# Transposing x on VectorE and by way of DRAM in a one-core decoder layer

## The chip, the cores and the metric

One NeuronCore of a Trainium2 chip runs the whole program; there is no communication. The metric is the device time of one execution in microseconds; the time of a kernel is the median of its runs. Everything is 32-bit floating point. Engines are named as in the profile: PE is TensorE (PEld its weight loads), DVE is VectorE, ACT is ScalarE, POOL is GpSimd, and SP only issues DMAs.

## What is computed

One decoder layer on x of 16 batches, 512 tokens and 256 channels, in three residual blocks, each closed by a layer norm. The change touches the first:

```python
q  = x + x @ Wq + bq                       # 16 heads of 16 channels
ks = x + x @ Wk[k] + bk[k]                 # k = 0, 1
vs = x + x @ Wv[k] + bv[k]
state = prod over k of (ks[k].T @ vs[k]) / 1024    # per batch and head, 16 x 16
out = LayerNorm(q @ state) @ Wo + bo
x = LayerNorm(x + out)
```

The second block is cross-attention to 64 context tokens with 16 heads; the third is a mixture of eight experts with a capacity of 1024 tokens each, which the inputs give to the first two batches.

## The kernel before, in words

The keys and values of the linear attention are never formed. For each batch the kernel makes the Gram matrix of x over the tokens, with a column of ones beside the channels (`gram`, L544), and gets the states out of it by small products with the weights (`self_attention`, L608: `g_times_wk`, `states`). Tokens lie on the partitions there, so the tile `gx` is x as it stands in memory: four tiles of 128 tokens, 257 columns. Since the Gram matrix sums over tokens, their order within a batch doesn't matter to it. `load_gram_x` (L293) loads it two batches ahead into two buffers; `grams_of` runs up to five batches ahead of the states.

The queries do need x with channels on the partitions. `self_attention(b)` loads x a second time into `xt` (L605) and `transposed` (L227) turns it: eight 128x128 transposes on PE (L233) into two PSUM banks, which ACT and DVE copy out in turn (`evac`, L186 and L188) into `xT`. The query weights and the state are multiplied into one 256x264 matrix `m` (L664, evacuated at L668), and `ps_o` (L681) is x times `m`, token tile by token tile, with the router's columns beside the channels. Norm, another transpose (`zT`, L694), the product with `Wo` (L705), residual and norm follow; `xt` is the residual. `xT` and `zT` take turns in one buffer. The result goes to cross-attention (`ps_sim` L808, softmax over DVE, ACT and POOL, block transposes on DVE at L798, `ps_x` L828) and to the routing.

For the first two batches the experts run as a stream of their own (`ps_h` L940, `ps_e` L957), cut into pieces that fill PE's time from about 200 us on. `ranks` (L869) checks at the end whether later batches belong to the experts as well; they don't here, and the loop at L1151 runs no turns.

The order of the work is written by a planner inside the kernel. Each part is a generator; `Model` (L28) keeps a book of when each tile is made and each engine free by fixed costs per instruction, and `weave` (L1004) always takes the ready stream that is most behind its due time. A `yield WAIT` lets a stream rest until what it issued is done, and `until(...)` until a condition holds. `in_order` (L1023) then fixes this order on PE, DVE, ACT and POOL. DMAs are all issued by SP, which takes its queue in order. PSUM has eight banks of 512 floats, shared by all parts in turn.

Before the steady state lies a setup of some 110 us: the context's keys (`ps_kv` L436, 16 pairs of matmuls whose results go by way of two buffers `st` each to `k_dram`), the values times the output weights (`ps_vo` L486), the router's weights (`ps_rw` L379), and the first four Gram matrices.

Of the kernel before, what the change touches and what calls it, by code (L numbers as in the profile page):

```python
# [9 lines left out]
FP = mybir.dt.float32  # L10
# [3 lines left out]
ALU = mybir.AluOpType  # L14
# [4 lines left out]
P = 128  # L19
# [5 lines left out]
WAIT = "wait"  # L25


class Model:  # L28
# [37 lines left out]
    def run(self):  # L66

        traced = self.nc.cur_bb.bb.instructions
        end = now = self.free.get("PE", 0.0)
        self.took = 0.0  # L70
        for ins in traced[self.seen:]:
            kind, engine = type(ins).__name__, str(ins.engine).split(".")[-1]
            aps = [[a.bass_ap for a in l if hasattr(a, "bass_ap")] for l in (ins.ins, ins.outs)]
            names = [[a.name for a in l] for l in aps]
            at = 0.0
            for made, used, l in ((1, 0, names[0]), (1, 1, names[1])):
                for n in l:
                    if kind == "InstDMACopy" and self.made.get(n, (0, 0))[1] == "SP":
                        continue
                    for known, book in ((made, self.made), (used, self.used)):  # L80
                        if known and n in book:
                            t, by = book[n]
                            at = max(at, t + (self.WIDE.get(by, 0.0) if by != engine else 0.0))
            if kind == "InstDMACopy":
                size = 4 * min(a.size() for l in aps for a in l)
                start = max(at, self.dma if now < 40 else 0.0)
                self.dma = start + size / 220e3
                done = self.dma + 2.0
            elif names[1]:
                start = max(at, self.free.get(engine, 0.0))  # L90
                done = self.free[engine] = start + self.duration(ins, kind, engine)
                if engine == "PE":
                    self.took += done - start
                else:
                    end = max(end, done + 0.15)
            else:
                continue
            for n in names[0] + names[1]:
                self.used[n] = max(self.used.get(n, (0.0, None)), (done, engine), key=lambda p: p[0])
            for n in names[1]:  # L100
                self.made[n] = (done, engine)
        self.seen, self.end = len(traced), end
        return end

# [12 lines left out]
def decoder_layer(  # L117
# [25 lines left out]
    nc = tc.nc  # L143

    B, S, C = x.shape
    J = context.shape[1]
    NT = S // P
    NC = C // P
# [4 lines left out]
    NP = INNER // P  # L153
# [7 lines left out]
    QB = 4  # L161
# [20 lines left out]
    def evac(dst, src):  # L182

        flip[0] ^= 1
        if flip[0]:
            nc.scalar.copy(dst, src)  # L186
        else:
            nc.vector.tensor_copy(dst, src)  # L188
# [30 lines left out]
    w_sel = const.tile([P, NTT, E], FP, tag="w_sel", name="w_sel")  # L219
# [7 lines left out]
    def transposed(dst, src, view=lambda t: t, ones=False):  # L227


        for cc in range(NC):  # L230
            ps = bank("ps_t")
            for t in range(NT):
                nc.tensor.transpose(ps[:, t * P:(t + 1) * P], src[:, t, cc * P:(cc + 1) * P], ident)  # L233
            v = view(dst[:, cc, :])
            ps = ps if len(v.shape) == 2 else ps.rearrange("p (q t i) -> p q t i", q=NT, t=NT)
            if ones and cc == NC - 1:
                nc.vector.tensor_scalar(v, ps, not_last, ident[:, P - 1:P], ALU.mult, ALU.add)
            elif ones:
                nc.scalar.copy(v, ps)
            else:  # L240
                evac(v, ps)

    def moments(NT=NT):

# [27 lines left out]
    with ExitStack() as att:  # L272
# [17 lines left out]
        wk1 = pool(att, "wk1", 1)  # L290
        wk2 = pool(att, "wk2", 2)

        def load_gram_x(b, eng=nc.sync, pieces=1):  # L293

            t = gp.tile([P, NT, C + 1], FP, tag="gx", name="gx")
            nc.gpsimd.memset(t[:, :, C:], 1.0)
            n_ = NT // pieces
            for i in range(pieces):
                eng.dma_start(
                    out=t[:, i * n_:(i + 1) * n_, :C],  # L300
                    in_=x[b, i * n_ * P:(i + 1) * n_ * P, :].rearrange("(t p) c -> p t c", p=P),
                )
            return t

        gram_x = {0: load_gram_x(0, pieces=NT)}
# [138 lines left out]
        def context_keys():  # L444

            cT = held["cT"] = sp.tile([P, NC, BJ], FP, tag="cT", name="cT", bufs=1)
            held["wT"] = {}
            for q in range(BJ // 512):
                transposed(cT[:, :, q * 512:(q + 1) * 512], nats.pop(0))
                nats.append(load_wkv(sp, q))  # L450
                yield WAIT
            for r4 in range(2 * NP // 4):
                nat = nats.pop(0)
                wT = held["wT"][r4] = sp.tile([P, NC, 512], FP, tag="wT", name="wT")
                transposed(wT, nat)
                if r4 + 2 < 2 * NP // 4:
                    nats.append(load_wkv(sp, r4 + 2))
                yield WAIT
                if r4 >= NP // 4:
                    continue  # L460
                for r in range(r4 * 4, r4 * 4 + 4):
                    for q in range(BJ // 512):
                        st = context_rows(r, q)
                        nc.sync.dma_start(
                            out=k_dram[q * NG:(q + 1) * NG, :, r, :].rearrange("g p t -> p g t"),
                            in_=st.rearrange("p (g t) -> p g t", g=NG),
                        )
                        yield
            nc.sync.dma_start(out=xwq, in_=x_wq.rearrange("(r p) c -> p r c", p=P))

            last = small.tile([P, NP], FP, tag="last", name="last")
# [70 lines left out]
        def gram(b, u4):  # L544
# [22 lines left out]
            nc.tensor.transpose(ps[:, :P], g[:, 1, :], ident)  # L567
            evac(g[:, 3, :], ps[:, :P])
            grams[b] = g
            yield WAIT  # L570

        def key_sums(u4):
# [25 lines left out]
                    sums[b // QB][1].append(key_sums(sums["u4"]))  # L598
                    yield WAIT

        grams, sums = {}, {}

        def load_x(b):
            t = wk1.tile([P, NT, CX], FP, tag="xt", name="xt")
# [3 lines left out]
        def self_attention(b, done):  # L608
# [5 lines left out]
            gks = []  # L614

            def g_times_wk(k):

# [36 lines left out]
            state = wk1.tile([P, NC, P], FP, tag="state", name="state")  # L654
            nc.vector.tensor_mul(state, sk[:, 0], sk[:, 1])
            nc.vector.scalar_tensor_tensor(state, state, STATE_SCALE, headmask, ALU.mult, ALU.mult)
            yield from until(lambda: made(xt))
            transposed(xT, xt)
            yield WAIT

            ps = bank("ps_m")
# [11 lines left out]
                )  # L673
            nc.scalar.copy(bq_state[:, :C], ps[:, :C])
            yield WAIT
            z = wk1.tile([P, NT, CX], FP, tag="z", name="z")
            mm = moments()
            for t in range(NT):
                ps = bank("ps_o")
                for cc in range(NC):  # L680
                    nc.tensor.matmul(  # L681
                        ps[:, :CX], xT[:, cc, t * P:(t + 1) * P], m[:, cc, :], start=(cc == 0), stop=(cc == NC - 1)
                    )
                nc.vector.tensor_add(z[:, t, :], ps[:, :CX], bq_state)
                moment(mm, t, z[:, t, :])
                yield
# [182 lines left out]
        def ranks():  # L869
# [36 lines left out]
            least = small.tile([P, NB], FP, tag="least", name="least")  # L906
# [153 lines left out]
        def all_self_attention():  # L1060
            for b in range(B):
                self_st.plan(SETUP + (b - 1) * STEP, STEP, 16.5)
                yield from until(lambda: b in grams and sums[b // QB][1] and "rb" in cs and made(grams[b], sums[b // QB][1][0]))
                yield from self_attention(b, done)

        def all_context():
# [84 lines left out]
    with tc.For_i(0, n, 1) as i:  # L1151
        acc = fw.tile([P, NT, C], FP, tag="acc", name="acc")
        nc.sync.dma_start(out=acc, in_=x2_rest[ds(i * S, S), :].rearrange("(t p) c -> p t c", p=P))
        wb = fw.tile([P, NT, E], FP, tag="wb", name="wb")
        nc.vector.tensor_copy(wb, w_sel[:, ds(i * NT + HEAD_B * NT, NT), :])
        aT = fw.tile([P, NC, S], FP, tag="aT", name="aT")
        transposed(aT, acc)
        for e in range(E):
# [44 lines left out]
```

## Time and profile before

| | |
|---|---|
| median of three runs | 1394.06 us (1392.28 to 1394.08) |
| profiled execution | 1391.12 us |
| its span in the profile | 1389.4 us, 24206 instructions |
| mean granted PE clock | 0.995 of full speed |
| DMA | 153.57 MB in 98373 packets, engines busy 40% |

The profile shows one execution. Busy time is the sum of an engine's instructions; matmuls are pipelined, so their records overlap. A 32-bit matmul has two records, a transpose one. For each group of instructions the page gives line, engine, operation, output<-input, shapes and number, then busy us and the mean ns of one, then the engine's idle time just before them and what ended most of it. Waits are listed by the line that waited and the line that released it.

Of DVE's 850.5 us and ACT's 402.2 us most lies in the softmax, the norms and the evacuations. Of the DMAs, 512 issues of 132 KB load `vo`, the largest share; x is loaded twice, as `gx` and as `xt`, 512 KB a batch each.

### The profile page before, as it was taken

The numbers are of one execution on the slowest core, as the hardware profiler recorded it, in microseconds if no ns is written. First come the engines' busy times: TensorE is split into PE (matmuls) and PEld (weight loads), VectorE is DVE, ScalarE is ACT, GpSimd is POOL, SyncE is SP. The second block draws the span as 40 slices with busy tenths as digits, with TensorE's granted clock in tenths as the row PEclk, the third lists the DMA queues.
The fourth block names the chain that finished last, engine by engine and source line by source line (L and its number), as shares of the span: only waits on it lengthen the run. The fifth ranks groups of instructions, "written<-read, shape, count | busy, mean of one in ns | idle before, by whom it ended". The sixth has DMA issues, their size and how long they took to land.

```text
span 1389.4 us, 24206 instructions
## 1 busy us (share of the span) xinstructions
PE 1363.8 (98%) x9630; PEld 1075.8 (77%) x9630; DVE 850.5 (61%) x1957; ACT 402.2 (29%) x912; POOL 203.9 (15%) x140
## 2 busy tenths in 40 slices
PE   7999999999999999999999999999999999999997
PEld 4666676877878787878878787878888787878686
DVE  2345848466583848476584848475675939484744
ACT  1134323132232314142233223142323323232322
POOL 0001112112020111112020112112020202111200
PEclk9999999999999999999999999999999999999999
DMA  8657775511516153421606053513334061505211
GB/s 261 202 121 193 201 188 169 141 32 33 154 46 157 46 141 106 123 80 47 186 18 169 31 141 106 126 62 75 112 94 124 16 187 46 147 26 126 91 55 40
DMA packets 98373, 153.57 MB, mean 111 GB/s; under 512 B 15561, under 2 KB 70097, under 8 KB 98257
## 3 DMA queue, kind: packets, MB, share of 16 engines
q1 hardware_dynamic: 98256, 151.98, 39.9%
q8 instruction: 78, 1.28, 0.4%
q14 instruction: 39, 0.31, 0.1%
HBM read 114.71 MB, written 37.22 MB: 109 GB/s over the span
## 4 chain that ended last, share of the span: by engine, by line
PE 90%; DVE 6%; DMA 2%; ACT 1%; issue 0%; SPq 0%; DVEq 0%; ACTq 0%
PE ps_x L828 17%; PE ps_sim L808 15%; PE ps_e L957 15%; PE ps_h L940 14%; PE ps_p L705 4%; PE ps_gk L623 4%; PE ps_o L681 3%; PE ps_kv L436 3%; PE ps_t L233 2%; PE ps_vo L486 2%; PE ps_kq L745 2%; PE ps_s L635 2%; PE ps_g L549 2%; PE ps_zt L694 1%; PE ps_m L664 1%; PE ps_g L554 1%
## 5 line engine op out<-in xcount | busy, mean ns | idle before, releaser
L940 PE MATMUL ps_h<-head_T,wi 128*128 128x256 f32 x1024 | 239.1, 379 | 0.0
L828 PE MATMUL ps_x<-vo,pT 32*128 32x264 f32 x4096 | 234.4, 385 | 3.7 <-DVE pT L798 3.7
L808 PE MATMUL ps_sim<-kq,x1T 128*128 128x512 f32 x512 | 235.0, 593 | 0.0
L828 PEld LDWEIGHTS ps_x<-vo,pT 32*128 32x128 f32 x4096 | 212.5, 186 | 24.5 <-issue 5.6
L940 PEld LDWEIGHTS ps_h<-head_T,wi 128*128 128x128 f32 x1024 | 193.4, 190 | 38.8 <-issue 13.0
L796 POOL TENSOR_TENSOR s<-s,sm 128x1024 f32<-128x1024 f32 x64 | 121.8, 1903 | 539.1 <-DVE sm L795 500.7
L835 DVE TENSOR_TENSOR x<-ps_x,x 128x264 f32<-128x264 f32 x64 | 23.2, 426 | 225.6 <-PE ps_x L828 225.6
L816 ACT ACTIVATE s<-s 128x512 f32<-128x512 f32 x128 | 80.7, 630 | 276.0 <-DVE s L815 276.0
L808 PEld LDWEIGHTS ps_sim<-kq,x1T 128*128 128x128 f32 x512 | 94.5, 190 | 83.2 <-issue 74.2
L814 DVE TENSOR_REDUCE mx<-ps_sim 128x8 f32<-128x512 f32 x128 | 86.1, 672 | 42.2 <-PE ps_sim L808 41.9
L815 DVE TENSOR_TENSOR s<-ps_sim,mx 128x512 f32<-128x512 f32 x128 | 88.5, 692 | 4.4
L719 POOL TENSOR_TENSOR x<-x,bout 128x1056 f32<-128x1056 f32 x16 | 38.8, 2422 | 320.9 <-ACT hT L946 172.6
L798 DVE STREAM_TRANSPOSE pT<-s 128x1024 f32<-128x1024 f32 x64 | 78.6, 1228 | 7.0 <-POOL s L796 7.0
L946 ACT ACTIVATE hT<-ps_h 128x256 f32<-128x256 f32 x128 | 47.0, 377 | 119.9 <-PE ps_h L940 119.7
L695 ACT ACTIVATE zT<-ps_zt,shift,gain 128x512 f32<-128x512 f32 x32 | 23.2, 776 | 189.7 <-PE ps_zt L694 189.7
L794 DVE TENSOR_REDUCE sm<-s 128x16 f32<-128x1024 f32 x64 | 77.1, 1204 | 0.4 <-ACT s L816 0.4
L267 ACT ACTIVATE x<-x,off,rstd 128x264 f32<-128x264 f32 (+1 forms) x112 | 58.3, 591 | 29.3 <-DVE off L265 29.3
L681 PE MATMUL ps_o<-m,xT 128*128 128x264 f32 x256 | 66.7, 387 | 0.0
L261 ACT ACTIVATE rstd<-bn_mv,eps 128x4 f32<-128x4 f32 (+1 forms) x70 | 20.7, 295 | 158.6 <-DVE bn_mv L250 155.1
L948 DVE TENSOR_SCALAR hT<-ps_h 128x256 f32<-128x256 f32 x128 | 52.1, 409 | 22.5 <-PE ps_h L940 22.3
L705 PE MATMUL ps_p<-wo,zT 128*128 128x264 f32 x256 | 63.1, 387 | 0.0
L436 PE MATMUL ps_kv<-cT,wT 128*128 128x512 f32 x128 | 61.1, 612 | 0.2 <-ACT vst L186 0.2
(172 smaller groups left out, 1892.6 us busy)
## 6 DMA issues: line engine op xcount, KB each, us to landing
vo<-vo_dram SPq DMA_DIRECT2D x512, 132.0 KB, 4.1
vo_dram<-vst SPq DMA_DIRECT2D x128, 132.0 KB, 2.4
xt<-in_x_dram SPq DMA_DIRECT2D x16, 512.0 KB, 4.0
wi<-L_ffn_experts_inter_dram SPq DMA_DIRECT2D x8, 1024.0 KB, 5.1
gx<-in_x_dram SPq DMA_DIRECT2D x15, 512.0 KB, 4.2
x_rest<-x SPq DMA_DIRECT2D x14, 512.0 KB, 3.0
out_dram<-x SPq DMA_DIRECT2D x14, 512.0 KB, 2.9
k_dram<-st SPq DMA_DIRECT2D x16, 256.0 KB, 3.5
```

The lines of the kernel that those rows point to most:

```text
L436: nc.tensor.matmul(ps, wT[:, cc, r % 4 * P:(r % 4 + 1) * P], cT[:, cc, q * 512:(q + 1) * 512], start=(cc == 0), stop=(cc == NC - 1),)
L681: nc.tensor.matmul(ps[:, :CX], xT[:, cc, t * P:(t + 1) * P], m[:, cc, :], start=(cc == 0), stop=(cc == NC - 1))
L705: nc.tensor.matmul(ps[:, :CX], zT[:, cc, t * P:(t + 1) * P], wo[:, cc, :], start=(cc == 0), stop=(cc == NC - 1))
L796: nc.gpsimd.tensor_mul(s, s, sm.unsqueeze(2).to_broadcast([P, NH, J]))
L798: nc.vector.transpose(probsT[:, :, t, :], s.rearrange("p h (a j) -> p (h a) j", a=2))
L808: nc.tensor.matmul(ps, x1T[:, cc, t * P:(t + 1) * P], kq[:, cc, hf * 512:(hf + 1) * 512], start=(cc == 0), stop=(cc == NC - 1),)
L814: nc.vector.tensor_reduce(mx[:, hs], sim, AX.X, ALU.max)
L815: nc.vector.tensor_sub(s[:, hs, :], sim, mx[:, hs].unsqueeze(2).to_broadcast([P, 8, J]))
L816: nc.scalar.activation(s[:, hs, :], s[:, hs, :], AF.Exp, scale=SCALE)
L828: nc.tensor.matmul(ps[q][:, :CX], probsT[pq, blk].rearrange("p t i -> p (t i)"), vos[c][pq, i, :], start=(c == 0 and i == 0), stop=(c == 7 ...
L940: nc.tensor.matmul(ps[:, :TB], wi[:, cc, f * P:(f + 1) * P], head_T[b][:, cc, t0 * P:t0 * P + TB], start=(cc == 0), stop=(cc == NC - 1),)
L957: nc.tensor.matmul(ps[:, :C], hT[f][:, t * P:(t + 1) * P], wo_[:, f, :], start=(f == 0), stop=(f == NF - 1),)
```

## The change

`w_sel` is dropped (its values go into `w_all`), which together with single buffers for `last` and `least` makes room for a tile `xb`. For batch 0 everything else stays. For batches 1 to 15:

- `gx` is loaded in another order of tokens, by four DMAs of 32 partitions each instead of one of 128.
- Behind the batch's Gram matrix DVE transposes `gx` in 32x32 blocks (`to_blocks`, four instructions), and ACT issues a DMA of the blocks to a DRAM tile `x_blocks[b]`. Only then is the next `gx` loaded into the same pair of buffers.
- `self_attention(b)` begins with four DMAs, issued by ACT (`from_blocks`), that read the blocks into `xT` with channels on the partitions. PE's transposes of `xt` and their two evacuations are gone; `xt` is still loaded for the residual.
- `ps_o` reads `xT` in another layout, and waits in the plan until it is there.
- The planner's book reckons 0.35 us of ACT for a DMA issue of ACT and 5 us until it has landed.

```diff
@@ Model.run
-            if kind == "InstDMACopy":
+            if kind == "InstDMACopy" and engine == "Activation":
+                start = max(at, self.free.get(engine, 0.0))
+                self.free[engine] = start + 0.35
+                done = start + 5.0
+            elif kind == "InstDMACopy":
@@ new
+    def to_blocks(src):
+        xb = wk1.tile([P, NT, NC, NT, 32], FP, tag="xb", name="xb")
+        for q in range(NT):
+            nc.vector.transpose(
+                xb[:, :, :, q, :].rearrange("p k c j -> p c k j"),
+                src[:, q, :C].rearrange("p (c k j) -> p c k j", c=NC, j=32),
+            )
+        return xb
+
+    def from_blocks(dst, there):
+        for k in range(NT):
+            nc.scalar.dma_start(
+                out=dst[k * 32:(k + 1) * 32].rearrange("i t c n -> i t (c n)"),
+                in_=there[:, :, k, :].rearrange("t i n -> i t n"),
+            )
@@ load_gram_x
+                else:
+                    eng.dma_start(
+                        out=t[i * 32:(i + 1) * 32, :, :C],
+                        in_=x[b, i * P:(i + 1) * P, :].rearrange("(q j) c -> j q c", j=32),
+                    )
@@ gram
-            if b + 2 < B:
-                gram_x[b + 2] = load_gram_x(b + 2)
...
             grams[b] = g
+            if b > 0:
+                yield WAIT
+                xb = to_blocks(gx)
+                yield WAIT
+                x_blocks[b] = dram.tile([NT, 32, NT, NC * P], FP, tag=f"x_blocks{b}", name="x_blocks")
+                nc.scalar.dma_start(
+                    out=x_blocks[b].rearrange("t i k n -> (t i) (k n)"), in_=xb.rearrange("p k c q j -> p (k c q j)")
+                )
+            if b + 2 < B:
+                gram_x[b + 2] = load_gram_x(b + 2)
@@ self_attention
-            xT = wk1.tile([P, NC, S], FP, tag="xT", name="xT")
+            xT = wk1.tile([P, NT, NC, P], FP, tag="xT", name="xT")
+            if b > 0:
+                from_blocks(xT, x_blocks.pop(b))
...
-            yield from until(lambda: made(xt))
-            transposed(xT, xt)
+            if b == 0:
+                yield from until(lambda: made(xt))
+                transposed(xT.rearrange("p t c n -> p c t n"), xt, lambda t: t)
...
+            yield from until(lambda: made(xT))
...
-                        ps[:, :CX], xT[:, cc, t * P:(t + 1) * P], m[:, cc, :], start=(cc == 0), stop=(cc == NC - 1)
+                        ps[:, :CX], xT[:, t, cc], m[:, cc, :], start=(cc == 0), stop=(cc == NC - 1)
@@ ranks
-            nc.vector.scalar_tensor_tensor(w_sel, rank, float(CAP), w_all, ALU.is_lt, ALU.mult)
+            rest = slice(HEAD_B * NT, NTT)
+            nc.vector.scalar_tensor_tensor(
+                w_all[:, rest], rank[:, rest], float(CAP), w_all[:, rest], ALU.is_lt, ALU.mult
+            )
```

Since every part is planned anew, instructions far from these lines stand in another order too.

More of the change, by code (lines that the diff above doesn't have):

```diff
@@ L98, in run @@
             for n in names[0] + names[1]:
-                self.used[n] = max(self.used.get(n, (0.0, None)), (done, engine), key=lambda p: p[0])
+                by = "SP" if kind == "InstDMACopy" else engine
+                self.used[n] = max(self.used.get(n, (0.0, None)), (done, by), key=lambda p: p[0])
             for n in names[1]:
-                self.made[n] = (done, engine)
+                self.made[n] = (done, "SP" if kind == "InstDMACopy" else engine)
         self.seen, self.end = len(traced), end
@@ L218, in decoder_layer @@
     NTT = B * NT
-    w_sel = const.tile([P, NTT, E], FP, tag="w_sel", name="w_sel")
     n_i = const.tile([P, 1], I32, tag="n_i", name="n_i")
@@ L234, in transposed @@
             v = view(dst[:, cc, :])
-            ps = ps if len(v.shape) == 2 else ps.rearrange("p (q t i) -> p q t i", q=NT, t=NT)
+            if len(v.shape) > 2:
+                ps = ps.rearrange("p (q n) -> p q n", n=P) if len(v.shape) == 3 else ps.rearrange(
+                    "p (q t i) -> p q t i", q=NT, t=NT
+                )
             if ones and cc == NC - 1:
@@ L291, in decoder_layer, with load_gram_x @@
         wk2 = pool(att, "wk2", 2)
-        def load_gram_x(b, eng=nc.sync, pieces=1):
+        def load_gram_x(b, eng=nc.sync, pieces=NT):
             t = gp.tile([P, NT, C + 1], FP, tag="gx", name="gx")
@@ L298, in load_gram_x @@
             for i in range(pieces):
[L299 to L302, printed above, removed]
+                if b == 0:
+                    eng.dma_start(
+                        out=t[:, i * n_:(i + 1) * n_, :C],
+                        in_=x[b, i * n_ * P:(i + 1) * n_ * P, :].rearrange("(t p) c -> p t c", p=P),
+                    )
+                else:
+                    eng.dma_start(
+                        out=t[i * 32:(i + 1) * 32, :, :C],
+                        in_=x[b, i * P:(i + 1) * P, :].rearrange("(q j) c -> j q c", j=32),
+                    )
             return t
@@ L469, in context_keys @@
             nc.sync.dma_start(out=xwq, in_=x_wq.rearrange("(r p) c -> p r c", p=P))
-            last = small.tile([P, NP], FP, tag="last", name="last")
+            last = small.tile([P, NP], FP, tag="last", name="last", bufs=1)
             nc.vector.tensor_copy(last, xwq[:, :, C - 1])
@@ L569, in gram @@
             grams[b] = g
+            if b > 0:
[5 more added lines that the diff above has]
+                    out=x_blocks[b].rearrange("t i k n -> (t i) (k n)"), in_=xb.rearrange("p k c q j -> p (k c q j)")
+                )
+            if b + 2 < B:
+                gram_x[b + 2] = load_gram_x(b + 2)
             yield WAIT
@@ L599, in grams_of @@
                     yield WAIT
-        grams, sums = {}, {}
+        grams, sums, x_blocks = {}, {}, {}
         def load_x(b):
@@ L612, in self_attention @@
             sk = wk1.tile([P, K, NC, P], FP, tag="sk", name="sk")
-            xT = wk1.tile([P, NC, S], FP, tag="xT", name="xT")
-            gks = []
+            xT = wk1.tile([P, NT, NC, P], FP, tag="xT", name="xT")
+            if b > 0:
+                from_blocks(xT, x_blocks.pop(b))
             def g_times_wk(k):
@@ L656, in self_attention @@
             nc.vector.scalar_tensor_tensor(state, state, STATE_SCALE, headmask, ALU.mult, ALU.mult)
-            yield from until(lambda: made(xt))
-            transposed(xT, xt)
+            if b == 0:
+                yield from until(lambda: made(xt))
+                transposed(xT.rearrange("p t c n -> p c t n"), xt, lambda t: t)
             yield WAIT
@@ L903, in ranks @@
             nc.vector.tensor_add(rank, rank, start)
-            nc.vector.scalar_tensor_tensor(w_sel, rank, float(CAP), w_all, ALU.is_lt, ALU.mult)
+            rest = slice(HEAD_B * NT, NTT)
+            nc.vector.scalar_tensor_tensor(
+                w_all[:, rest], rank[:, rest], float(CAP), w_all[:, rest], ALU.is_lt, ALU.mult
+            )
             NB = B - HEAD_B
-            least = small.tile([P, NB], FP, tag="least", name="least")
+            least = small.tile([P, NB], FP, tag="least", name="least", bufs=1)
             nc.vector.tensor_reduce(
@@ L1062, in all_self_attention @@
                 self_st.plan(SETUP + (b - 1) * STEP, STEP, 16.5)
-                yield from until(lambda: b in grams and sums[b // QB][1] and "rb" in cs and made(grams[b], sums[b // QB][1][0]))
+                yield from until(
+                    lambda: b in grams and sums[b // QB][1] and "rb" in cs and made(grams[b], sums[b // QB][1][0])
+                    and (b == 0 or b in x_blocks and made(x_blocks[b]))
+                )
                 yield from self_attention(b, done)
@@ L1154, in decoder_layer @@
         wb = fw.tile([P, NT, E], FP, tag="wb", name="wb")
-        nc.vector.tensor_copy(wb, w_sel[:, ds(i * NT + HEAD_B * NT, NT), :])
+        nc.vector.tensor_copy(wb, w_all[:, ds(i * NT + HEAD_B * NT, NT), :])
         aT = fw.tile([P, NC, S], FP, tag="aT", name="aT")
```

## The prediction

> **What bounds the kernel now.** I read the page's busy times first, then the grid of slices, then who TensorE waited for, then TensorE's timeline around the transposes in question, then the setup in windows.
>
> ```profile
> PE 1363.8 (98%) x9630; PEld 1075.8 (77%) x9630; DVE 850.5 (61%) x1957; ACT 402.2 (29%) x912; POOL 203.9 (15%) x140
> PEclk9999999999999999999999999999999999999999
> ```
>
> TensorE works for all but 25.6 of 1389.4 us; no other engine comes near. So an instruction taken off TensorE shortens the run by its own length, unless something else is then late. The waits filtered to TensorE say how close that is:
>
> ```profile
> PE ps_x L828 <- DVE pT L798: 3.7, 2, 3.2
> PE ps_rw L379 <- DVE early L376: 3.3, 1, 3.3
> PE ps_t L233 <- DMA nat<-in_L_xattn_Wkv_dram: 3.1, 1, 3.1
> PE ps_g L549 <- DMA gx<-in_x_dram: 3.0, 1, 3.0
> PE ps_e L957 <- DVE hT L948: 1.8, 1, 1.8
> ```
>
> (columns: total us, times, longest.) Three of the five, 9.4 us, lie in the first 32 us; behind it there is hardly a wait. The stages from 200 us to 1300 us are filled by the planner with expert matmuls, so there a microsecond off TensorE counts in full. TensorE's timeline around one transposition of x:
>
> ```profile
> 229.53 1.03 PE L940 MATMUL ps_h<-head_T,wi 128*128 128x256 f32 x4
> 230.40 1.04 PE L233 MATMUL ps_t<-ident,xt 128*128 128x128 f32 x8
> 231.27 3.60 PE L808 MATMUL ps_sim<-kq,x1T 128*128 128x512 f32 x8
> ```
>
> The records overlap, so the price is start to start: 231.27 - 230.40 = 0.87 us for eight. Fourteen of the sixteen batches show 0.86 to 0.89, the first two 0.96.
>
> **Removed.** For batches 1 to 15 the eight transposes go: 120 instructions. The built order of the changed kernel has exactly 120 fewer matmuls, all of this kind, and as many changes between 128, 64 and 32 rows as before (81), so nothing is added at the seams. 14 x 0.87 + 0.96 = 13.1 us off TensorE. Their evacuations also go, 15 on DVE and 15 on ACT:
>
> ```profile
> L188 DVE COPY xT<-ps_t 128x512 f32<-128x512 f32 x16 | 10.9, 683 | 0.0
> L186 ACT COPY xT<-ps_t 128x512 f32<-128x512 f32 x16 | 9.2, 575 | 3.2 <-PE ps_t L233 3.2
> L798 DVE STREAM_TRANSPOSE pT<-s 128x1024 f32<-128x1024 f32 x64 | 78.6, 1228 | 7.0 <-POOL s L796 7.0
> ```
>
> **Added on VectorE.** 60 block transposes of 128x256. The nearest row is the last one: 1228 ns for 1024 elements, also written with a stride; taking 80 ns of it as fixed, 256 elements cost 0.37 us. 60 x 0.37 - 15 x 0.68 = +12 us on an engine with 539 us idle. They stand behind the Gram matrices, several batches ahead of need; the cover is DVE's idle third. Without cover four in a row delay what stands behind them by 1.5 us.
>
> [...]
>
> **Added in DMA.** Per batch one write of 512 KB and four reads of 128 KB, 15 MB on 153.57 MB: the DMA share goes from 40% to about 44%. The reads are issued at the start of self_attention(b) and first needed by ps_o. Adding up the matmuls between in the built order at their rows gives 15 us in the three tightest batches and 23 to 35 in the others, against about 4 us for the comparable loads (xt 4.0, gx 4.2 from issue to landing). Hidden; with the cover gone it is 4 us a batch.
>
> **Added in ACT's queue.** The write and the reads are issued by ACT, 75 issues. No DMA issue on ACT is in the trace; the nearest row is SP's: 0.39 us alone, 17.56 / 32 = 0.55 in a burst of vo loads. So 75 x 0.39 to 0.55 = 29 to 41 us, less 15 x 0.575 = 9 us of copies: ACT goes from 29% to about 31%. What matters is the block of four reads, 1.6 to 2.2 us, with kq copies, Exp or hT queued behind it. [...] By the row it is half the landing time, on an engine that computes. In the built order TensorE reaches ps_e 3.5 to 5 us of matmul work after the hT that ACT evacuates, and the planner already reckons 0.35 us an issue, so an overrun of some 0.6 us should mostly be absorbed. From 0 (all absorbed) to 5 us (a third of a microsecond per batch); a gain is excluded, since copies worth 0.6 us leave and 2.0 to 2.75 us come. I take 1, near the absorbed end.
>
> Each DMA also takes one of eight landing counters in turn and waits until that counter's previous DMA, possibly SP's, has landed. In the built order no such wait hangs on later TensorE work than ACT has already waited for; the closest (batch 2, behind the xt load) leaves 4.9 us of matmuls for a landing of 4.0.
>
> **Moved: the loads of gx.** For b > 0 four issues instead of one: 45 more on SP, and they now wait for DVE's transposes as well as for ps_g. Later gx loads are needed tens of microseconds on; queued behind them are vo loads with 9 us of reserve. In the setup it is tighter. Windows of 6 us:
>
> ```profile
> 6.00:12.00 6.00, 5.38 (x35) 4.23 (x34) 1.65 (x7) 1.77 (x4) 0.10 (x1) 1.00 1.10 338
> 12.00:18.00 6.00, 2.86 (x20) 2.21 (x19) 2.06 (x6) 0.64 (x2) 0.11 (x1) 1.00 1.03 345
> 24.00:30.00 6.00, 3.87 (x10) 1.39 (x8) 1.23 (x2) 0.78 (x2) 0.00 (x0) 1.00 0.97 283
> 30.00:36.00 6.00, 4.83 (x13) 3.56 (x14) 1.13 (x5) 0.00 (x0) 0.00 (x0) 0.72 0.63 167
> ```
>
> (PE, PEld, DVE, ACT, POOL busy; clock; DMA share; GB/s.) The DMA engines are full where TensorE waits for nat, so three more issues before it (3 x 0.51 us) delay it by 0 to 1.5, taken 1.0: the issue is late, but the transfers are the limit. ps_rw waits for DVE, which sits behind k_dram stores; the new order puts 8 ps_kv instead of 6 before it, four transposes into DVE's queue and gx behind them into SP's, ahead of two stores: -0.5 (two more matmuls cover) to +3, taken 1.0. The fourth Gram matrix has 6.6 us of matmuls for four issues and a landing of 4.2 behind two stores: 0 to 2, taken 0.5. Sum 2.5 us, from -0.5 to 6.5. A longer wait here costs twice: the last window shows the clock at 0.72 after the 3.3 us wait.
>
> **Moved: everything else.** The planner decides again. In the new order four places take a PSUM bank with little work since it was used (a kq or g copy 0.2 to 1.1 us of matmuls earlier, where the copy alone is 0.28 to 0.68 us and queues): about 0.5 us each, 2 us, from -3.7 (the pT waits could vanish) to 5; I take 2 because the places can be named. At the end, DVE's rank sums delay hT (1.8 us); the new order has 14 ps_h matmuls instead of 10 between ps_in and that wait, 1.7 us more cover: -0.7, from -1.5 to 0. w_sel's merging into w_all is one instruction, slightly shorter: nothing.
>
> **Sum.** -13.1 + 1 + 2.5 + 2 - 0.7 = -8.3 us. The profiled execution took 1391.1 us, 1.7 outside its span; this would be 1382.8. The runs' median is 1394.06, 2.9 above the profiled one, so on the median 1394.06 - 8.3 = **1385.8 us**.
>
> **The rivals.** Under 0.2% (2.8 us) a measurement of this kernel cannot be told from no change.
>
> *Nearly all of the gain arrives* (0.18): the re-planned order costs nothing, the setup's extra issues lie in the shadow of full DMA engines. -13.1 - 0.7 = 1380.3. For it: TensorE has no wait worth the name from 200 to 1300 us. Against it: the tight banks.
>
> *The setup eats it* (0.12): nat, ps_rw and the Gram load at their upper ends, 6.5 us with the clock penalty of 1.6, and the banks at 4: -13.1 + 8.1 + 4 = -1.0, 1393.1. For it: the setup is where waits are; against: only 35 us of it.
>
> *ACT's queue becomes the bound* (0.08, slower): at the four reads of self_attention(b), ACT waits for another DMA's landing, 4.1 us, and then issues, 2.75: 6.9 us in which no bank is emptied by ACT. TensorE's reserve is about 4.3, so it loses 2.6 us; in every second batch 7 x 2.6 = 18 us, 1385.8 + 18 = 1404. From (8.3 + 2.8) / 15 = 0.74 us per batch on, the change is slower than before. For it: a computing engine now waits in order on DMAs. Against: the built order has them landing long before.
>
> The forecast itself has 0.62, its own range 1380.5 to 1391. That the transposes stay is excluded by the built order.
>
> **How the numbers follow.** Faster 0.80 (the forecast and the full gain), same 0.12, slower 0.08. The range, 1378.5 to 1394.5, takes in the bounds of the unknown terms except their coinciding, the full gain, and the case of the setup; above it lies ACT's case.
>
> **What would show it.** ps_t<-ident,xt in one batch only; TensorE's busy time down by about 15 us as its records count (each 1.04 us a group, overlapping); 60 transposes into xb near 370 ns; DMA issues on ACT near 0.4 to 0.55 us; TensorE's waits at 20 to 26 us, more of them before 40 us. Wrong if TensorE waits for hT, kq or s of ACT by more than 5 us in total, if ps_o waits for xT, or if SP stands behind gx while ps_x waits for vo.

## The result, and the profile after

The changed kernel takes 1405.29 us (median of six runs, 1403.26 to 1409.26); beside it the kernel before took 1393.52 us. The ratio is 1.0092, 95% interval 1.0074 to 1.0109: 12.8 us slower by the ratio (11.8 by the two medians), where 8.3 us faster was forecast, and outside the range. The profiled execution took 1404.68 us (before 1391.12), its span is 13.6 us longer.

The page of the changed kernel, busy times and granted clock:

```profile
PE 1360.0 (97%) x9510; PEld 1065.4 (76%) x9510; DVE 849.9 (61%) x2002; ACT 395.5 (28%) x897; POOL 203.6 (15%) x140
PEclk9999998999999999999999999999999999999999
```

TensorE has 120 instructions fewer, but only 3.8 us less busy time, and it is idle for 43.0 us instead of 25.6. Busy time counts overlapping records once, so 13.1 us less were due, and not the 15 that the forecast got by adding up the records. The slice with clock 8 (210 to 245 us) lies in the stage in which most of the new idle time arose. Whom TensorE waited for (total us, times, longest):

```profile
PE ps_g L583 <- DMA gx<-in_x_dram: 5.3, 2, 3.1
PE ps_t L237 <- ACT x L294: 3.9, 4, 3.4
PE ps_vo L520 <- ACT vst L191: 3.5, 5, 1.9
PE ps_rw L413 <- DVE early L410: 3.5, 1, 3.5
PE ps_vo L520 <- DVE s L860: 3.1, 3, 2.0
PE ps_gt L599 <- ACT g L191: 3.0, 1, 3.0
PE ps_gt L599 <- DVE g L193: 2.4, 1, 2.4
```

The waits for gx and ps_rw lie before 40 us, the wait for g of DVE at 350 us; of the others all but 0.4 us lie between 150 and 250 us: with 0.7 us for x_head 13.8 us, where the kernel before had 2.2. What follows such waits stands in the windows of 10 us there (PE, PEld, DVE, ACT, POOL busy; clock; DMA share; GB/s):

```profile
220.00:230.00 10.00, 6.53 (x33) 5.40 (x32) 8.02 (x28) 1.92 (x7) 0.10 (x1) 1.00 0.85 196
230.00:240.00 10.00, 5.73 (x19) 3.61 (x20) 2.38 (x9) 4.89 (x12) 2.40 (x1) 0.57 1.06 249
240.00:250.00 10.00, 10.00 (x30) 6.04 (x29) 6.36 (x14) 1.15 (x2) 0.00 (x0) 0.91 0.87 235
```

After 3.5 us of idle the clock is 0.57 in the next window: of the 5.7 us that look busy there some 2.5 (5.73 x 0.43, an estimate) are the same matmuls taking longer. Added up over windows of 5 us, busy time times what is missing of the full clock, the clock costs 8.9 us in the changed kernel and 4.2 before. These 4.7 us are half of the 9.3 by which busy time fell short; the other half stays open (in e3 below, where only the transposes are gone, it falls short by 3.4).

What the change touches itself looks as forecast: the transposes of xt are there for batch 0 only (eight), the block transposes take 412 ns, a DMA issue of ACT 0.34 us for a write and 0.44 for a read, and the landings (last column of the page's DMA rows, us) are short:

```profile
L257 DVE STREAM_TRANSPOSE xb<-gx 128x256 f32<-128x256 f32 x60 | 21.2, 412 | 2.8 <-DMA x_blocks<-xb 2.8
x_blocks<-xb ACTq DMA_DIRECT2D x15, 512.0 KB, 3.1
xT<-x_blocks ACTq DMA_DIRECT2D x60, 128.0 KB, 3.1
```

The simplest landmark is the start of ps_x, which comes once per batch. How much later than before TensorE reaches it, in us, worked out from the traces (some of the runs below are in the table too). Each row is one profiled execution, and executions of one kernel differ: 45 of the kernel before lay between 1388.2 and 1395.5 us, the one profiled of e5 is 2.2 us above the median of its kernel, that of e6 3.8 below. The runs e1 to e18 are described in the next section:

| kernel | batch 0 | 1 | 4 | 8 | 15 |
|---|---|---|---|---|---|
| changed | 13.0 | 22.3 | 18.5 | 19.5 | 11.4 |
| old order, no transposes (e3) | 1.2 | 1.1 | -1.3 | -4.7 | -9.7 |
| new order alone (e5) | 13.9 | 17.6 | 12.8 | 13.8 | 5.0 |
| new order, no trip (e1) | 16.9 | 22.8 | 18.0 | 19.0 | 10.9 |
| old order, no trip (e6) | 1.5 | 4.1 | 3.1 | -0.4 | -5.4 |
| old order, all new work (e4) | 5.0 | 14.6 | 18.1 | 15.6 | 11.7 |
| old order, from batch 8 (e13) | 1.5 | 2.2 | 3.4 | 1.7 | -2.3 |

The changed kernel is 22.3 us late at batch 1. From there to batch 15 it makes up 10.9 us, as the one with the bare transposes left out does (10.8), but 2.6 us of that (an estimate from the rows of ps_h) are not a gain: 12 matmul records of the experts that stood ahead of ps_x of batch 15 now stand behind it. At batch 1 what is done otherwise weighs about the same (16 expert records more, 16 Gram records fewer). So some 8.3 of the 10.8 us arrive, about three quarters; TensorE's idle time between the two landmarks is 6.9 us instead of 3.7, the 2.4 us of the wait for g at 350 us among it.

### The profile page after: what moved, and what is told of

It is laid out like the page before. It is cut to its first block, busy times and chain, and to the rows that moved or that the text cites. A ratio compares the mean times of both kernels' runs of the same rounds, so it can differ in the third digit from the quotient of the medians.

```text
span 1403.0 us, 24179 instructions
## 1 busy us (share of the span) xinstructions
PE 1360.0 (97%) x9510; PEld 1065.4 (76%) x9510; DVE 849.9 (61%) x2002; ACT 395.5 (28%) x897; POOL 203.6 (15%) x140
## 4 chain that ended last, share of the span: by engine, by line
PE 83%; DVE 8%; DMA 5%; SPq 2%; ACT 1%; issue 1%; POOL 0%; DVEq 0%; ACTq 0%; POOLq 0%
PE ps_x L873 15%; PE ps_h L988 14%; PE ps_e L1005 14%; PE ps_sim L853 13%; PE ps_p L750 4%; PE ps_gk L666 4%; PE ps_o L726 3%; PE ps_kv L470 3%; PE ps_kq L790 2%; PE ps_vo L520 2%; PE ps_s L678 2%; PE ps_g L583 1%; PE ps_t L237 1%; DVE pT L843 1%; DVE sm L839 1%; SPq L525 1%
## 5 line engine op out<-in xcount | busy, mean ns | idle before, releaser
L666 PE MATMUL ps_gk<-wk,g 128*128 128x256 f32 x256 | 61.8, 388 | 0.0
```

What stands on the lines that cost most here:

```text
L666: nc.tensor.matmul(ps[:, :C], blk, wk[:, j, k, :], start=(j == 0), stop=(j == NC - 1))
```

## The experiments

The planner answers to any edit with another order, so an edit of the source changes two things at once. To change one, the planner's choices were written down (which stream goes next, and whether a condition held) and replayed in another kernel. "New order" is that of the changed kernel, "old order" that of the kernel before:

```diff
         def weave():
             model.run()
-            while streams:
-                ...
-                st = min(now, key=Stream.time)
-                wait = next(st.gen, "end")
+            every = list(streams)
+            for i in range(0, len(PICKS), 2):
+                known = len(streams)
+                st = every[int(PICKS[i:i + 2], 16)]
+                wait = next(st.gen, "end")
+                model.run()
+                every += streams[known:]
```

"us" below is the ratio to the kernel before on the same chip less 1, times 1393. A difference of two rows carries both intervals, some 2 to 4 us together; the terms below are to be read so. In e1, e3, e5, e6, e15, e17 and e18 part of the work is left out.

| run | ratio (95%) | us |
|---|---|---|
| changed kernel | 1.0092 (1.0074 to 1.0109) | +12.8 |
| e1 new order, no trip | 1.0075 (1.0058 to 1.0092) | +10.4 |
| e2 new order, trip by SP | 1.0114 (1.0082 to 1.0146) | +15.9 |
| e3 old order, no transposes | 0.9906 (0.9889 to 0.9922) | -13.1 |
| e4 old order, all new work | 1.0105 (1.0082 to 1.0128) | +14.6 |
| e5 new order alone | 1.0018 (1.0011 to 1.0025) | +2.5 |
| e6 old order, no trip | 0.9991 (0.9981 to 1.0002) | -1.3 |
| e7 from batch 4, planned | 1.0089 (1.0066 to 1.0112) | +12.4 |
| e8 from batch 4, old order | 1.0033 (1.0021 to 1.0045) | +4.6 |
| e9 from batch 7, old order | 1.0012 (1.0003 to 1.0021) | +1.7 |
| e10 from batch 7, planned | 0.9989 (0.9980 to 0.9999) | -1.5 |
| e11 before, replanned a | 1.0057 (1.0039 to 1.0075) | +7.9 |
| e12 before, replanned b | 1.0007 (0.9993 to 1.0022) | +1.0 |
| e13 from batch 8, old order | 0.9972 (0.9963 to 0.9980) | -3.9 |
| e14 from batch 8, planned | 0.9974 (0.9966 to 0.9982) | -3.6 |
| e15 new order, one step moved | 1.0034 (1.0022 to 1.0045) | +4.7 |
| e16 old order, trip by SP | 1.0078 (1.0060 to 1.0096) | +10.9 |
| e17 gx in pieces alone | 0.9953 (0.9939 to 0.9966) | -6.5 |
| e18 block transposes alone | 0.9947 (0.9929 to 0.9965) | -7.4 |

### Is it ACT's queue, or the order? (e1 to e4)

From the waits two theories could be read: ACT, which now issues DMAs and waits for landings (A), or the new order (B). Without the trip:

```diff
-                nc.scalar.dma_start(
-                    out=x_blocks[b].rearrange("t i k n -> (t i) (k n)"), in_=xb.rearrange("p k c q j -> p (k c q j)")
-                )
...
-                from_blocks(xT, x_blocks.pop(b))
...
-                        ps[:, :CX], xT[:, t, cc], m[:, cc, :], start=(cc == 0), stop=(cc == NC - 1)
+                        ps[:, :CX], xT[:, t, cc] if b == 0 else xt[:, t, cc * P:(cc + 1) * P], m[:, cc, :],
+                        start=(cc == 0), stop=(cc == NC - 1),
```

> The changed kernel with every engine's order kept as planned, but without the trip by way of DRAM: the write of x_blocks and the four reads of xT (75 DMA issues on ACT, 15 MB) are left out, and ps_o takes the untransposed x for batches 1 to 15, so its values mean nothing. VectorE's block transposes, the pieces of gx and their order stay. Theory A, ACT's queue: issues on ACT wait for landings and hold up the evacuations behind them; then without them the time falls by nearly all of the missing 20 us, to 1385 to 1390. Theory B, the order: the planner's new order leaves TensorE without ready work in the setup and from 150 to 250 us, whatever ACT issues; then only the one wait of 3.0 us for g behind ACT's issue and its clock dip go, and the time is 1398 to 1402.

Measured +10.4 us (1403.8), just above the range of B. The trip costs 2.4 us in the new order, which the two intervals do not tell from nothing. A falls for the changed kernel. With `nc.sync` instead of `nc.scalar` for the trip:

> The changed kernel with the orders of TensorE, VectorE, ACT and POOL kept, but the write and the reads of the trip are issued by SP instead of ACT. Theory A (ACT's queue): ACT is free, about 1386 to 1392, unless SP's own queue becomes late. Theory B (the order): 1399 to 1406, since TensorE's waits for DVE and for the setup stay.

+15.9 us: no gain from an ACT free of issues. Now the bare price, the old order with `transposed(xT, xt)` for batch 0 only, and ps_o reading xt as above:

> The kernel before, every engine's order kept, with TensorE's transposes of x for batches 1 to 15 and their evacuations simply left out: ps_o takes the untransposed x, so its values mean nothing. This is the price of the removed part alone. Both theories: 13.1 us less than before, 1381; if other waits take up part of it, up to 1386.

-13.1 us, the sum of the transposes (with an interval of 2.3 us to either side, the last digit is luck). All the new work in the old order, without yields and conditions of its own:

```diff
-                yield WAIT
                 xb = to_blocks(gx)
-                yield WAIT
...
-            yield from until(lambda: made(xT))
```

> All of the change's work (block transposes on VectorE, the trip issued by ACT, gx in four pieces behind them), in the order in which the planner of before put the rest: the new instructions stand where their step stood, and the order of the others is that of the kernel before. Theory A (ACT's queue): the issues on ACT still hold up the evacuations, 1396 to 1405. Theory B (the order): 1382 to 1389, the removed transposes less some small waits.

+14.6 us (1405.7), at the upper end of A's range, so B fails in its pure form too: in the old order the change is as slow as in the new one, by another way. Its trace shows how. First ACT's timeline (start, duration; in brackets the idle time before):

```profile
221.71 0.34 ACTq L653 DMA_DIRECT2D x_blocks<-xb  x1
222.10 0.30 ACT L336 ACTIVATE rstd<-bn_mv,eps 128x4 f32<-128x4 f32 x1 [2.59 <-DMA vo<-vo_dram]
```

ACT's write has its data and stands still until a vo load, issued by SP, has landed; g is evacuated behind it, and TensorE waits 2.4 us for g. Then SP's queue and TensorE:

```profile
225.22 7.92 SPq L381 DMA_DIRECT2D gx<-in_x_dram  x8
234.22 0.45 SPq L1067 DMA_DIRECT2D wi<-L_ffn_experts_inter_dram  x1
241.26 1.76 PE L1033 MATMUL ps_h<-head_T,wi 128*128 128x256 f32 x4 [5.00 <-DMA wi<-L_ffn_experts_inter_dram]
```

Eight pieces of gx stand ahead of the first expert's weights. The second four come behind VectorE's block transposes, which wait 1.2 us for ACT's write to land, since xb has one buffer; SP itself waits 4.4 us among them for other landings (2.3 for gx, 2.1 for xT). Before, wi was issued at 220.35 us; here at 234.22, and the first expert matmul waits 5.0 us.

### Splitting the sum (e5, e6, e17, e18, e16)

The new order with none of the new work (the trip is left out as in e1, and gx comes in the token order of before):

```diff
-        def load_gram_x(b, eng=nc.sync, pieces=NT):
+        def load_gram_x(b, eng=nc.sync, pieces=1):
...
+            if b + 2 < B:
+                gram_x[b + 2] = load_gram_x(b + 2)
             g = gp.tile([P, 4, P], FP, tag="g", name="g", bufs=5)
...
                 yield WAIT
-                xb = to_blocks(gx)
                 yield WAIT
...
-            if b + 2 < B:
-                gram_x[b + 2] = load_gram_x(b + 2)
```

> The changed kernel's order alone: every engine keeps the order that the planner chose for the change, but VectorE's block transposes, the trip by way of DRAM and the pieces of gx are left out; gx is loaded by one DMA right after its Gram matrix, as before. As in the runs without transposes ps_o takes the untransposed x, so its values mean nothing. Theory B (the order itself leaves TensorE waiting; the run without the trip, 1404, still held it): 1398 to 1404. Theory C (the block transposes, and gx loaded in pieces behind them, are what delays): 1380 to 1385, as the kernel before without its transposes (1380).

+2.5 us (1395), between the two expectations. Against -13.1 for the old order, the order costs 15.6 us; neither B nor C is the whole. The old order with transposes and pieces but no trip:

> The old order with the block transposes and the pieces of gx, but without the trip by way of DRAM (ps_o takes the untransposed x, so its values mean nothing). With the trip this order took 1406. Theory C (transposes and pieces): 1398 to 1404. Theory D (in an order that was planned without it, the trip's issues on ACT cost some 20 us; the new order avoids that and loses as much by its own waits): 1381 to 1387.

-1.3 us (1391), between C and D. Transposes and pieces cost 11.8 us in the old order and 7.9 in the new (e1 less e5); the trip 15.9 in the old (e4 less e6) and 2.4 in the new. The sum for the changed kernel is -13.1 + 15.6 + 7.9 + 2.4 = 12.8 us; it closes by construction, since each term is the difference of one run and the next. In the planner's order the trip is cheap and the order dear; in the old one it is the other way round.

The pieces alone (four DMAs, other token order, issued where the one was), and the block transposes alone (one DMA in token order, behind them):

> The old order without transposes of x (1380), with one part of the change added: gx of batches 1 to 15 comes in four pieces and in the other token order, issued where it was, right after its Gram matrix. No block transposes, no trip, and ps_o takes the untransposed x, so its values mean nothing. With the block transposes too it took 1391. If the pieces in SP's queue cost those 11 us: 1387 to 1391. If the block transposes and the loads behind them do: 1380 to 1383.

> The other part alone: the old order without transposes of x, with the block transposes on VectorE, and gx loaded by one DMA in the order of before, but behind them, as in the change. Values mean nothing here either. If the pieces cost the 11 us: 1380 to 1384. If the block transposes and the load (with its memset on POOL) moved behind them do: 1385 to 1391.

6.6 and 5.7 us more than e3: together 12.3, against 11.8 for both. Neither part carries the price alone. By the ps_x landmark the pieces have lost their share by batch 1 (6.0 us late, e3 1.1); the transposes lose theirs between batch 0 (1.9 us early, e3 1.2 late) and batch 2 (2.3 late, e3 0.2). Of the 5.7 us for the transposes, 2.5 are one wait of TensorE for `off` of VectorE at 252 us, the wait that in e9 follows a VectorE instruction of 2.19 instead of 0.19 us beside GpSimd (last section), with the clock at 0.66 in the 5 us behind it. Every old-order run with block transposes of batch 7 has this wait (e4, e6, e8, e9, e16, e18), and e3, e13 and e17 don't.

> All of the change's work in the old order (1406 with the trip issued by ACT, 1391 without the trip), with the write and the reads issued by SP. If the trip's 15 us in this order are ACT's, which waits for landings with g and Exp behind it: 1390 to 1395. If they are SP's and the DMA engines' (expert weights and vo late): 1402 to 1409.

+10.9 us (1401), near the second expectation: ACT's part of the trip's 15.9 is 3.7 us. Most of the other 12.2 is again the late wi, whoever issues the trip: it is issued at 234.64 us, TensorE waits 6.1 us for it, and in the 7 us behind that the clock is 0.51, another 3.4 us.

### What in the new order costs (e15), and whether any new order does (e11, e12)

VectorE's timeline of the new order alone (e5), the end of batch 0's softmax:

```profile
178.34 1.10 DVE L244 COPY vst<-ps_vo 128x264 f32<-128x264 f32 x3
...
185.99 1.77 DVE L244 COPY vst<-ps_vo 128x264 f32<-128x264 f32 x4 [4.44 <-PE ps_vo L571]
187.68 1.24 DVE L889 STREAM_TRANSPOSE pT<-s 128x1024 f32<-128x1024 f32 x1
188.83 1.18 DVE L885 TENSOR_REDUCE sm<-s 128x16 f32<-128x1024 f32 x1
...
199.86 0.43 DVE L244 COPY vst<-ps_vo 128x264 f32<-128x264 f32 x1 [5.06 <-DMA vo_dram<-vst]
...
202.30 1.24 DVE L889 STREAM_TRANSPOSE pT<-s 128x1024 f32<-128x1024 f32 x1
```

and the same steps in the old order (e3):

```profile
176.93 1.21 DVE L848 STREAM_TRANSPOSE pT<-s 128x1024 f32<-128x1024 f32 x1
178.06 1.18 DVE L844 TENSOR_REDUCE sm<-s 128x16 f32<-128x1024 f32 x1
...
189.46 1.23 DVE L848 STREAM_TRANSPOSE pT<-s 128x1024 f32<-128x1024 f32 x1
```

In the new order eight evacuations of value products stand in VectorE's queue ahead of the last row sum and the last two pT. They wait for TensorE, whose clock is 0.50 from 180 to 185 us, and later ones for stores to land, while softmax data lies ready: the last row sum comes 10.8 us later, the last pT 12.8 us, and ps_x of batch 0 starts at 204.40 instead of 191.71 us. 2.1 us of this shift are eight more value products done by then; the rest is lost. In the whole span TensorE is idle for 35.9 us in e5 and for 25.4 in e3, and the clock, added up as above, costs 10.8 and 5.6 us: 10.5 + 5.2 us, which is the order's price within the spread of single executions. By batch 1 nearly all of it has been lost (16.5 us, with as much work done).

Another reading was that TensorE lacks work in reserve: the old order has eight value products left behind ps_x and ps_p, the new none, and it waits there for x. One step was moved, in the replayed list:

```diff
- ps_vo (last), ps_x, ps_p, ...
+ ps_x, ps_p, ps_vo (last), ...
```

> The run of the new order alone (1395; no transposes of x, no trip, no block transposes, its values mean nothing) with one step moved: the last eight value products (ps_vo, 2.1 us) go from before the first ps_x to behind ps_p, where the old order had them. In the new order TensorE has only ps_p and a Gram matrix, 6.8 us, between ps_x and the transposes of x that need its result, and waits 2.6 us with a clock dip behind it. If the lack of such work in reserve is what the new order loses by: 1389 to 1393. If the place of this step does not matter: 1394 to 1397.

+4.7 us, not less than e5: that reading falls. ps_x now waits 2.56 us for pT instead. This agrees with the chain through VectorE as the limit of the stage. That the chain is the cause is read from the traces and not shown by a run: moving the softmax steps themselves was not tried.

Is the new order bad, or is nearly any? The kernel before, with one constant of the planner's book altered:

```diff
-            return 0.09 + n * 1.035e-3 ...
+            return 0.10 + n * 1.035e-3 ...
```

> The kernel before, with all its work and nothing added; only the planner reckons 0.10 us instead of 0.09 us as the fixed part of each VectorE instruction, so it chooses another order in 15 places before 430 us and more behind. If almost any other order of the crowded stage is worse than the one before had: 1397 to 1408. If the order of the change was bad by itself, and not orders in general: 1390 to 1395.

> The kernel before with all its work; only the planner reckons 0.13 us instead of 0.11 us for a transpose on TensorE, so it chooses another order in 22 places before 430 us. Expected as for the other one: 1397 to 1408 if almost any other order is worse, 1390 to 1395 if the order of the change was bad by itself.

(In the second a transpose is reckoned at 0.13 us instead of 0.11.) +7.9 and +1.0 us with the work unchanged: one order as in the first expectation, one as in the second (and not clear of nothing: its interval runs from -1.0 to 3.1 us). From batch 4 on the planned order costs 7.8 us more than the old one (e7 less e8). So a re-plan that reaches the first 360 us cost 1.0, 7.8, 7.9 and 15.6 us in the four orders measured.

### Where the change pays (e7 to e10, e13, e14)

With `b > 0` replaced by `b >= LATE`, and earlier batches as before:

> The change for batches 4 to 15 only, planned anew by the planner: batches 1 to 3, whose Gram matrices belong to the setup, keep TensorE's transposes and the single load of gx. 12 x 0.87 = 10.4 us less on TensorE. If the losses lie in the setup and in the stage from 150 to 250 us that it disturbs (B or C there): 1383 to 1388. If each batch loses through ACT's queue (A): 1396 to 1403.

> The same change for batches 4 to 15, in the order of the kernel before. If the trip's issues on ACT cost wherever the order was not planned for them (D): 1394 to 1402. If only the setup and batches 1 and 2 suffer (C, or D in that stage alone): 1383 to 1388.

+12.4 us, worse than either expectation, and +4.6, as D: the stage that loses (150 to 360 us) already works on the Gram matrices of later batches, up to batch 7, so the setup's batches are not all that it touches.

> The change for batches 7 to 15 only, in the order of the kernel before: the first Gram matrix with a trip is reached near 430 us, behind the stage from 150 to 360 us in which all losses of the runs so far lie. 9 x 0.87 = 7.8 us less on TensorE. If the work itself is free where the experts' matmuls fill the gaps: 1384 to 1387. If each trip costs ACT or SP something in the steady stage too: 1390 to 1394.

> The same change for batches 7 to 15, planned anew: the planner's order is that of the kernel before up to about 430 us and differs behind it. If a new order hurts only where there are no experts to fill in: 1384 to 1388. If any new order costs (some 10 us, as in the first 360 us): 1393 to 1400.

+1.7 us, at the upper expectation, and -1.5, between the two: a gain of 7.8 nearly lost. By the landmark e9 is 4.1 us late at batch 1 and 7.1 at batch 2, and then makes up. Its first block transposes lie at 339 us and not near 430, as was expected, and at 254 us a VectorE instruction of 0.19 us takes 2.19 (last section).

> The change for batches 8 to 15 only, in the old order. With batch 7 in it, one block transposition and its write fell at 339 us and a moved memset on POOL at 252 us held up VectorE by 2 us, both in the crowded stage; from batch 8 on everything new lies behind 360 us. 8 x 0.87 = 7.0 us less on TensorE. If the crowded stage is where all losses lie: 1385 to 1388. If the steady stage pays too: 1390 to 1394.

> The same for batches 8 to 15, planned anew. The planner's choices up to some 430 us are those of before. If the crowded stage is where all losses lie, also those of a new order: 1385 to 1388. If a new order costs in the steady stage too: 1390 to 1396.

-3.9 and -3.6 us, with intervals below 1: both are faster than the kernel before, by about half of the 7.0 us. Behind the crowded stage most of it arrives: by the landmark e13 gains 5.7 us from batch 6 to batch 15 (3.4 late, 2.3 early), with the order of the other work as before and one new wait of 0.6 us, for kq near 919 us. e14 moves from 3.9 late to 3.1 early, but 16 expert records, some 3.4 us, have gone behind ps_x of batch 15, so its gain is about 3.6. Ahead of it, with one load of gx in pieces as the only new work, the two executions are 3.4 and 3.9 us late; how much of that is the spread of single executions these runs don't tell.

## Why the prediction was wrong

- **-13.1 us for the transposes: right.** -13.1 measured (e3). In the changed kernel about three quarters of it arrive behind batch 1 (8.3 of 10.8 us).
- **"Moved: everything else", 2 us, from -3.7 to 5: this step failed.** The new order alone costs 15.6 us (e5 less e3), by some 10.5 us of idle TensorE and 5.2 of lower clock, while the prediction reckoned with a lower clock in the setup only. The prediction looked in the built order for places where a PSUM bank is taken soon after its last use, and priced four of them at 0.5 us. It did not follow VectorE's queue in the stage from 150 to 250 us, where the steady state's cover, the expert matmuls, does not yet exist; the last pT comes 12.8 us later there. "From 200 us to 1300 us filled by the planner" was taken as cover for everything outside the setup; expert matmuls begin at 229.5 us before and at 252.5 in the changed kernel.
- **VectorE's transposes "hidden", gx and the setup 2.5 us, from -0.5 to 6.5: mis-sized.** Together 7.9 us in the new order and 11.8 in the old. The 0.37 us of one was nearly right (0.41), though its 80 ns of fixed time were an assumption; what the trace of before shows is that VectorE's records overlap by 80 ns (902 of 952 overlaps, to the nearest 10 ns). Half of the price are the pieces (6.6 us), half the transposes with the load and its memset behind them (5.7, both in the old order), of which 2.5 us are the wait for `off` at 252 us (in e9 with GpSimd's memset moved away), which no term had. Of the three waits named for the setup only one grew: ps_g from 3.0 to 5.3 us. ps_rw went from 3.3 to 3.5 and nat from 3.1 to 1.6, in single executions. The cover named for the transposes, VectorE's idle third, is an average over the span: VectorE is busy for 27.95 of the 30 us from 150 to 180 us in e3.
- **ACT's queue 1 us, from 0 to 5: right for the order that was built (2.4 us), within its error.** But the sentence that no landing counter hangs on later work was wrong at one place. The traces show the counters: all 909 DMA issues of SP and ACT tell of their landing by the same eight, 113 or 114 each, and 898 of them carry a wait for their own counter. The write at 234.35 us does: the vo load that SP issued at 229.97 has the same counter and has landed at 234.33, g waits behind the write on ACT (3.65 us idle, lines below), and TensorE 3.0 us for g. In an order not planned for it the trip costs 15.9.

```profile
234.35 0.34 ACTq L607 DMA_DIRECT2D x_blocks<-xb  x1
234.73 0.37 ACT L191 COPY g<-ps_g 128x256 f32<-128x256 f32 x1 [3.65 <-DMA vo<-vo_dram]
```

- **The tail -0.7 us: 0.4 measured** (the wait for hT is 1.4 us instead of 1.8).
- **The rivals.** ACT's queue as the bound gave 1404 us, close to the measured time, by a mechanism that didn't occur: its loss was to come in every second batch, but the kernel without the trip (e1) is as late at batch 1 and makes up as much to batch 15 (22.8 and 10.9 us late). That the number fits is luck. None of the three named signs of failure came up (0.5 us of waits for hT of ACT, none of ps_o for xT, no gx in SP's queue ahead of a vo that ps_x waited for). That the planner's new order could lose more than the change gains was a term of the sum and not a rival, with too narrow a range.
- **Open.** Why the planner put the value evacuations ahead of the softmax steps was not settled. Besides what the section on the change shows, the planner lets self_attention(b) begin only when x_blocks[b] is written (`and (b == 0 or b in x_blocks and made(x_blocks[b]))`) and books tiles moved by DMA under SP; which of these edits drew the new order no run tells.

## What to carry to other kernels

Where a planner or scheduler decides the order, an edit has two prices, its work and the re-plan; freeze the order and measure them apart, and before forecasting walk each in-order queue through the stage with the least cover, not only the busiest engine. An average of idle time is no cover in a stage where that engine is full. If a change pays in the steady state and loses in the crowded beginning, apply it only where it pays: here from batch 8 on, 3.9 us faster than before.

## What the runs showed of the hardware

**In the kernel before 36 VectorE instructions, all with two inputs in SBUF, took over 0.25 and up to 1.70 us longer than the median of their kind, each beside a GpSimd instruction.** In e9, VectorE and POOL:

```profile
253.76 2.34 POOL L793 TENSOR_TENSOR xt<-xt,bo 128x1024 f32<-128x1024 f32 x1
253.95 2.19 DVE L948 TENSOR_TENSOR w_all<-w_all,rm 128x32 f32<-128x32 f32 x1
256.07 0.41 DVE L242 COPY g<-ps_g 128x256 f32<-128x256 f32 x1
258.25 9.98 PE L922 MATMUL ps_x<-vo,pT 32*128 32x264 f32 x144 [2.47 <-DVE off L341]
```

and in the kernel before:

```profile
251.79 0.19 DVE L854 TENSOR_TENSOR w_all<-w_all,rm 128x32 f32<-128x32 f32 x1
251.94 0.11 POOL L296 MEMSET gx<- 128x4 f32 x1 [0.45 <-PE ps_g L554]
252.15 2.36 POOL L699 TENSOR_TENSOR xt<-xt,bo 128x1024 f32<-128x1024 f32 x1
```

The same instruction takes 0.19 us in the kernel before, where it starts 0.36 us ahead of POOL's, and 2.19 us in e9, where it starts 0.19 us behind it. In the kernel before, a memset of 0.11 us that the load of gx takes along stands ahead of POOL's, after 0.45 us idle for ps_g; moved behind the block transposes in e9, it is not there, POOL started first, and TensorE waited 2.5 us instead of 0.5. The 36 instructions lost 43.6 us in all. The 19 block transposes of `pT`, with one input, that ran more than half beside POOL took at most 0.013 us longer than their median. What makes the difference the traces don't show.

**The granted clock was mostly below 1.00 behind waits of TensorE of 2 to 4 us, though not behind each, and in 8 of the 20 traces also without one.** In windows of 5 us it is mostly 0.5 to 0.9 there: in the kernel before 0.66 from 30 us on, behind 3.3 us of idle, and 0.82 from 340 us on, behind 3.2; but 1.00 from 15 us on, behind 3.1 us, and in the changed kernel 1.00 behind the 2.4 us at 350 us. In the kernel before it is 0.66 from 75 to 80 us with TensorE busy throughout (0.50 from 76 to 78, 1.00 again from 79), behind 32 matmul records of 8 columns each (ps_wo, 70.95 to 75.4 us, with 8 transposes between). The same matmuls are followed by such a dip in 8 of the 20 traces, with TensorE busy in all 8, and by none in 11, the changed kernel and e3 among them (in the last one a wait came between); what decides it stays open.
